# Softmax sums of a causal cross-attention block taken from ScalarE's accumulator output

## The chip, the cores and the metric

The kernel runs on one core of a Trainium2 chip. The core has a matrix engine (TensorE, PE in the profile), VectorE (DVE), ScalarE (ACT), GpSimd (POOL) and SyncE (SP, which here only issues DMAs). Each engine works through its own instructions in order, and the engines wait for each other through semaphores. The metric is the device time of one execution in microseconds (us); lower is better.

## The reference

One post-norm transformer block with cross-attention: 128 batches of 128 tokens, model width 256, 16 heads of 16, hidden width 1024, all in float32. The mask lets a token see only earlier ones (`j < i`), and the first token's attention is set to zero.

```python
q = (query @ Wq + bq).reshape(b, s, N_HEADS, D_K).transpose(0, 2, 1, 3)
k, v = ...   # the same of the context, with Wk, bk and Wv, bv
scores = jnp.einsum('bhqd,bhkd->bhqk', q, k) / jnp.sqrt(jnp.float32(D_K))
scores = jnp.where(j < i + mask, scores, NEG_INF)       # mask = 0
attn = jax.nn.softmax(scores, axis=-1)
attn = attn.at[:, :, 0, :].set(0.0)
ctx = jnp.einsum('bhqk,bhkd->bhqd', attn, v)
x = layer_norm(query + ctx @ Wo + bo, ln1_g, ln1_b)
ffn = jax.nn.relu(x @ W1 + b1) @ W2 + b2
out = layer_norm(x + ffn, ln2_g, ln2_b)
```

## The kernel before

The batches are taken two at a time: 64 pairs, `NP = 64`, one step for each. The order of the instructions on every engine is written out by hand (a manual schedule), and the kernel is a software pipeline: `step(p)` computes the scores and the softmax of pair p, the projections of pair p + 1, weighs the values of pair p - 2, and runs the feed-forward layers of pairs p - 3 and p - 4. Pairs 0 to 6 have steps of their own (`third` to `sixth` among them); `step` runs for p = 7 to 63, 57 times. After it `behind` and the last lines drain the pipeline.

The scores of a pair are held with the tokens that ask on the 128 partitions, 64 of each of the two batches. There are two tiles, both in the SBUF tile `sm`: the high one (`hi = 1`, the later 64 tokens of each batch) has 16 heads of 128 columns, the low one (`hi = 0`, the earlier 64 tokens) 16 heads of 64 columns, since an early token sees no late one. The high scores lie in PSUM banks 0 to 3, four heads in each, the low ones in banks 6, 7, 4 and 5.

In `step`, the softmax of a pair goes like this:

- VectorE adds the mask (L390 for the low tile, L743 for the high one) and takes the row maximum of each head, negated: L747, four heads at a time from each bank of the high tile, and L754 for the whole low tile.
- ScalarE makes the exponentials head by head in `exponential_by_head` (L762), 16 for the high tile out of PSUM and 16 for the low tile in place, with the negated maximum as the bias.
- `sums` on VectorE (L421, L422) reduces the exponentials to a sum for each head and row and takes the reciprocals, in three calls: heads 0 to 7 and 8 to 15 of the high tile, and all 16 heads of the low tile. GpSimd multiplies the exponentials by the reciprocals (L423).
- VectorE transposes the weights in blocks (L436, three calls of `turn`), and SyncE's DMAs (`bring`, L451) carry the blocks to their places in `pT`, which `weigh` reads two steps later.

In VectorE's own order the step is: masks and maxima, the residual sum L538 with its statistics (L525, L526), the three calls of `sums`, the transpose of the normalised tokens `x` of pair p - 2 (`turn_x1`, L663), the transposes of the next tokens (L247, twice), the first `turn`, the five additions of the second feed-forward layer (`sum_of_seven`, L823 and L831), two more calls of `turn`, and the statistics of the second norm (L525, L526). Then the masks of the next step follow.

In ScalarE's order it is: `cxT` (L505), the 32 exponentials, the query projection (L272), the first norm's `x` (L554), the keys (L291), the values (L311, L316), the second norm (L591), and the hidden layer's eight ReLUs in pairs (L707).

TensorE's order is: the scores (L376), the projections of queries (L261), attention output (L512), keys (L261) and values (L301), the second feed-forward layer as seven products (L794), the first one (L699), and the weighing of the values (L483, L493).

Of the kernel before, what the change touches and what calls it, by code (L numbers as in the profile page):

```python
# [8 lines left out]
F32 = mybir.dt.float32  # L9
AF = mybir.ActivationFunctionType  # L10
ALU = mybir.AluOpType
AX = mybir.AxisListType

P = 128
# [5 lines left out]
def tile_cross_attention_block(  # L20
# [22 lines left out]
    nc = tc.nc  # L43
# [3 lines left out]
    H = 16  # L47
# [20 lines left out]
    small = ctx.enter_context(tc.tile_pool(name="small", bufs=2))  # L68
# [182 lines left out]
    def add_bo(p):  # L251
        st = states[p]
        st["xb"] = proj.tile([P, 2, D], F32, tag="xb", name=f"xb_{p}")
        nc.gpsimd.tensor_tensor(
            st["xb"], tokens_of[p // 2][:, p % 2 * 2 : p % 2 * 2 + 2], bov_r[:, None, :].to_broadcast([P, 2, D]), ALU.add
        )
# [102 lines left out]
    def scores_both(p):  # L359

        st = states[p]
        for hi in range(2):
            st["sps", hi] = [
                at_bank(r if hi else (6, 7, 4, 5)[r], f"pss{hi}_{p}_{r}") for r in range(NS)
            ]
            room(p, hi)
        one, two = (0, 1), (2, 3)
        for strips, hi, m in (
            (two, 0, 0), (one, 1, 0), (two, 0, 1), (one, 1, 1),
            (two, 1, 0), (two, 1, 1), (one, 0, 0), (one, 0, 1),  # L370
        ):
            n = P if hi else HP
            for s in range(2):
                for r in strips:
                    strip, first = slice(32 * r, 32 * r + 32), s * P
                    nc.tensor.matmul(  # L376
                        st["sps", hi][r][
                            s * HP : (s + 1) * HP, m * 2 * n : (m + 1) * 2 * n
                        ].rearrange("p (e j) -> p e j", e=2),
                        st["qT"][strip, m, first + hi * HP : first + hi * HP + HP],  # L380
                        st["kT"][strip, m, :, first : first + n],
                        start=True, stop=True,
                    )
# [29 lines left out]
    def sums(p, hi, part):  # L413

        st = states[p]
        sm = st["sm", hi]
        n = sm.shape[2]
        su = small.tile([P, H], F32, tag=f"su{hi}", name=f"su{hi}_{p}_{part.start}")
        rs = small.tile([P, H], F32, tag=f"rs{hi}", name=f"rs{hi}_{p}_{part.start}")
        su, rs = su[:, part], rs[:, part]  # L420
        nc.vector.tensor_reduce(su, sm[:, part, :], AX.X, ALU.add)  # L421
        nc.vector.reciprocal(rs, su)  # L422
        nc.gpsimd.tensor_tensor(  # L423
            sm[:, part, :], sm[:, part, :],
            rs[:, :, None].to_broadcast([P, part.stop - part.start, n]), ALU.mult,
        )
# [46 lines left out]
    def weigh(p):  # L473

        st = states[p]
        pT = st.pop("pT")
        pc = at_bank(7, f"pc_{p}") if p > 1 else bank(f"pc_{p}")

        for m in range(KC):
            for s in range(2):  # L480
                at = (m * 2 + s) * P
                for j in range(NS):
                    nc.tensor.matmul(  # L483
                        pc[32 * j : 32 * j + 32, at : at + HP],
                        st["vd"][:, s, 4 * m + j].rearrange("p e d -> p (e d)"),
                        pT[:, 2 * s : 2 * s + 2, H + 2 * j + m, :],
                        start=True, stop=True,
                    )
            for s in range(2):
                at = (m * 2 + s) * P  # L490
                for e in range(2):
                    for j in range(NS):
                        nc.tensor.matmul(  # L493
                            pc[32 * j : 32 * j + 32, at + HP : at + P],
                            st["vz"][:, s, 4 * m + j, 2 * e : 2 * e + 2, :].rearrange(
                                "p e d -> p (e d)"
                            ),
                            pT[:, 2 * s : 2 * s + 2, 4 * j + 2 * m + e, :],
                            start=(e == 0), stop=(e == 1),
                        )  # L500
        st["pc"] = pc

    def context(p):
        pc = states[p].pop("pc").rearrange("p (u i) -> p u i", i=P)
        nc.scalar.copy(cxT.rearrange("p m s i -> p (m s) i")[:, :, 1:], pc[:, :, 1:])  # L505
# [81 lines left out]
    def norm2(p):  # L587
        st = states[p]
        t2, sd, nb = st["t2"], st["sd", 2], st["nb", 2]
        for s in range(2):  # L590
            nc.scalar.activation(  # L591
                t2[:, s], t2[:, s], AF.Identity, bias=nb[:, s], scale=sd[:, s]
            )

    def finish(p):
        t2 = states[p]["t2"]
        nc.gpsimd.tensor_tensor(t2, t2, g2_r[:, None, :].to_broadcast([P, 2, D]), ALU.mult)
        nc.gpsimd.tensor_tensor(t2, t2, be2_r[:, None, :].to_broadcast([P, 2, D]), ALU.add)
# [6 lines left out]
    def store(p):  # L605
        nc.sync.dma_start(
            out[2 * p : 2 * p + 2].rearrange("b p d -> p b d"), states.pop(p)["t2"]
        )
# [144 lines left out]
        st = states[p]  # L753
        nc.vector.tensor_reduce(st["nmx", 0], st["sm", 0], AX.X, ALU.max, negate=True)  # L754

    def exponential_by_head(p, hi, heads):

        st = states[p]
        sm, nmx = st["sm", hi], st["nmx", hi]
        for h in heads:  # L760
            src = st["sps", 1][h // 4][:, h % 4 * P : h % 4 * P + P] if hi else sm[:, h, :]
            nc.scalar.activation(sm[:, h, :], src, AF.Exp, bias=nmx[:, h : h + 1], scale=1.0)  # L762

    wt = const.tile([P, 4, FC // 2, P], F32, tag="wt", name="wt")

# [8 lines left out]
    def combine_hidden(p, engines):  # L774

        st = states[p]
        h = st["hT"].rearrange("p (k e) (s t) -> p e s k t", e=2, s=2)
        hs = st["hS"] = ffn.tile([P, 4, FC // 2, P], F32, tag="hS", name=f"hS_{p}", bufs=1)
        one, two = engines
        one.tensor_tensor(hs[:, 0], h[:, 0, 1], h[:, 1, 1], ALU.add)  # L780
        two.tensor_tensor(hs[:, 2], h[:, 0, 0], h[:, 0, 1], ALU.subtract)
        one.tensor_tensor(hs[:, 1], hs[:, 0], h[:, 0, 0], ALU.subtract)
        two.tensor_tensor(hs[:, 3], h[:, 1, 0], hs[:, 1], ALU.subtract)
# [68 lines left out]
    for which, first in (("c", c_first[:, 0:2]), ("x", tokens_of[0][:, 0:2])):  # L852
        st = states[0]
# [17 lines left out]
    for m in range(KC):  # L871
# [6 lines left out]
        for e in range(2):  # L878
            if m == 0:
                nc.scalar.activation(  # L880
                    st["kT"][:, m, e, :], pk[:, :TP], AF.Identity,
                    bias=bkh[:, m, e : e + 1], scale=half[:, e : e + 1],
# [9 lines left out]
    for m in range(KC):  # L892
# [6 lines left out]
        if m == 0:  # L899
            nc.scalar.activation(  # L900
                st["qT"][:, m, :], pq[:, :TP], AF.Identity,
                bias=bqs_c[:, m : m + 1], scale=QSCALE,
# [11 lines left out]
    for which, first in (("x", tokens_of[0][:, 2:4]), ("c", c_first[:, 2:4])):  # L914
        st = states[1]
# [59 lines left out]
    def load_ahead(p):  # L975
        if p % 2 == 0 and p + 4 < NP:
            load([p + 4, p + 5], "x")
        if p % 2 == 1:
            if p + 3 < NP:
                load([p + 3, p + 4], "c")  # L980
            if 3 < p < NP - 1:
                load_tokens((p + 1) // 2)
# [137 lines left out]
    ONES, TWOS = range(HH), range(HH, H)  # L1120
# [91 lines left out]
    def step(p):  # L1212
        last = p == NP - 1
        weigh(p - 2)
        context(p - 2)
        scores_both(p)
        if p == 7:
            norm2(p - 6)
        combine_hidden(p - 4, POOL_ALONE)
        if p == 7:  # L1220
            finish(p - 6)
            store(p - 6)
        add_bo(p - 1)
        load_ahead(p)
        mask(p, 0, B)
        if last:
            mask(p, 0, A)
        mask_high(p, A)
        exponential_by_head(p, 1, ONES)
        mask_high(p, B)  # L1230
        exponential_by_head(p, 1, TWOS)
        if not last:
            mask(p, 0, A)
        low_maximum(p)
        exponential_by_head(p, 0, range(H))
        if not last:
            queries(p + 1)
        attention_out(p - 2)
        attention_sum(p - 2)
        attention_stats(p - 2)  # L1240
        shift(p - 2, 1)
        norm1(p - 2)
        if not last:
            keys(p + 1)
        values(p)
        values_out(p)
        norm2(p - 5)
        sums(p, 1, ONE)
        sums(p, 1, TWO)
        sums(p, 0, ALL)  # L1250
        turn_x1(p - 2)
        residual1(p - 3)
        second_by_seven(p - 4)
        hidden(p - 3, range(FC))
        if p + 2 < NP:
            tokens(p + 2, "x")
            tokens(p + 2, "c")
        turn(p, 1, 0)
        sum_of_seven(p - 4)
        turn(p, 1, 1)  # L1260
        turn(p, 0, 0)
        bring(p, nc.sync, LATE_FIRST[: len(EVERY) // (1 + last)])
        finish(p - 5)
        store(p - 5)
        stats(p - 4, states[p - 4]["t2"], 2)
        scale_and_shift(p - 4)
# [6 lines left out]
    for p in range(7, NP):  # L1273
        step(p)
# [25 lines left out]
    p = NP - 1  # L1300
# [16 lines left out]
    st = states[NP - 1]  # L1317
# [53 lines left out]
```

## Time and profile before

| | |
|---|---|
| time, two runs | 1526.21 and 1532.23 us, median 1529.22 |
| the profiled execution | 1528.67 us, its span 1527.0 us |
| TensorE matmul busy | 1514.3 us |
| VectorE busy | 1332.4 us |
| GpSimd busy | 1255.9 us |
| ScalarE busy | 1118.3 us |
| exponentials by head, L762 | 944 of 128 columns and 944 of 64 columns |
| sums, L421 | 192, of which 171 (3 in each of 57 steps) are in `step` |

The profile is of one execution. A busy time is the time in which an engine had an instruction in work; an engine that is in work for all of the span sets its length, while idle time of another engine costs nothing. In a list of groups, each row gives line, engine and operation, written and read tiles, shapes and count, and then busy time, mean duration of one in ns, and the idle time of the engine just before them with what ended it. In a timeline, a row gives start, duration, engine, line, operation and count of merged instructions, with idle time before it in brackets. Instructions of ScalarE overlap: the next one starts before the one in front has ended, so the distance from start to start is shorter than a duration.

### The profile page before, as it was taken

How to read it: one execution, taken by the hardware profiler on the slowest of the kernel's cores; microseconds unless marked ns; L12 is line 12 of the kernel's file. 1: busy time of each engine (PE TensorE's matmuls, PEld its weight loads, DVE VectorE, ACT ScalarE, POOL GpSimd, SP SyncE). 2: the span in 40 equal slices, each digit the busy share in tenths (PEclk: the TensorE clock that was granted, in tenths of full speed). 3: DMA queues.
4: the chain of work that ended last, by engine and by line, in shares of the span. 5: the costliest groups of instructions: out<-in, count | busy, mean ns of one | idle time of the engine just before them, and what ended most of it. 6: DMA issues, size and time to landing. Idle time of an engine off the chain costs nothing.

```text
span 1527.0 us, 47892 instructions
## 1 busy us (share of the span) xinstructions
PE 1514.3 (99%) x17926; PEld 1360.6 (89%) x17926; DVE 1332.4 (87%) x2498; ACT 1118.3 (73%) x3391; POOL 1255.9 (82%) x1282
## 2 busy tenths in 40 slices
PE   8999999999999999999999999999999999999998
PEld 7788998998989989989989899899899898998997
DVE  7989988988988988889889889889898898898885
ACT  5668777877877877778778778777777787787752
POOL 6876988888888888888888888888888888888883
PEclk9999999999999999999999999999999999999999
DMA  9356665555656656655556666566566566564441
GB/s 192 87 120 141 154 156 132 135 136 132 143 139 138 143 120 141 148 132 135 137 134 142 145 134 136 132 136 148 134 136 138 128 141 147 133 144 109 115 112 49
DMA packets 415285, 204.24 MB, mean 134 GB/s; under 512 B 282448, under 2 KB 383056, under 8 KB 415056
## 3 DMA queue, kind: packets, MB, share of 16 engines
q1 hardware_dynamic: 412768, 199.34, 56.7%
q8 instruction: 144, 2.36, 0.7%
q10 hardware_dynamic: 2288, 1.85, 0.5%
q14 instruction: 85, 0.70, 0.2%
HBM read 70.26 MB, written 33.29 MB: 68 GB/s over the span
## 4 chain that ended last, share of the span: by engine, by line
PE 94%; DVE 3%; POOL 1%; DMA 1%; issue 1%; ACT 0%; SPq 0%; POOLq 0%; DVEq 0%
PE ph L699 28%; PE py L794 14%; PE pz L794 10%; PE pq L261 7%; PE po L512 7%; PE pv L301 7%; PE pk L261 7%; PE pss L376 6%; PE pc L493 4%; PE pc L483 2%; DVE tb L436 1%; PE py L719 0%; DMA x1t<-tbx 0%; DVE sm L390 0%; DVE su L421 0%
## 5 line engine op out<-in xcount | busy, mean ns | idle before, releaser
L699 PE MATMUL ph<-x1T,w 128*128 128x256 f32 x2048 | 453.6, 380 | 0.7 <-DMA x1T<-x1t 0.7
L699 PEld LDWEIGHTS ph<-x1T,w 128*128 128x128 f32 x2048 | 385.0, 190 | 50.9 <-issue 1.2
L423 POOL TENSOR_TENSOR sm<-sm,rs 128x1024 f32<-128x1024 f32 x192 | 359.3, 1898 | 3.9 <-DVE rs L422 3.3
L762 ACT ACTIVATE sm<-pss,nmx 128x128 f32<-128x128 f32 x944 | 249.9, 414 | 127.3 <-DMA pT<-tb 81.0
L707 ACT ACTIVATE hT<-ph,b1e_c 128x256 f32<-128x256 f32 x504 | 209.1, 467 | 171.3 <-PE ph L699 161.3
L762 ACT ACTIVATE sm<-sm,nmx 128x64 f32<-128x64 f32 x944 | 232.2, 337 | 5.1 <-DVE nmx L754 0.3
L421 DVE TENSOR_REDUCE su<-sm 128x8 f32<-128x1024 f32 (+1 forms) x192 | 225.8, 1176 | 4.0 <-ACT sm L409 3.8
L436 DVE STREAM_TRANSPOSE tb<-sm 128x1024 f32<-128x1024 f32 x186 | 221.0, 1214 | 0.0
L390 DVE TENSOR_TENSOR sm<-pss,neg 128x256 f32<-128x256 f32 (+1 forms) x276 | 108.2, 435 | 121.2 <-PE pss L376 115.4
L532 POOL TENSOR_SCALAR ve<-mv 128x2 f32<-128x2 f32 x127 | 28.7, 226 | 191.7 <-DVE mv L526 190.9
L794 PE MATMUL py<-wt,hS 128*128 128x128 f32 x1440 | 170.6, 275 | 0.0
L794 PEld LDWEIGHTS py<-wt,hS 128*128 128x128 f32 x1440 | 165.7, 192 | 0.0
L747 DVE TENSOR_REDUCE nmx<-pss 128x4 f32<-128x512 f32 x236 | 150.8, 680 | 0.0
L261 PE MATMUL pq<-xT,wq 128*128 128x256 f32 x504 | 125.5, 392 | 0.5 <-DVE sm L390 0.5
L291 ACT ACTIVATE kT<-pk,bkh,half 128x256 f32<-128x256 f32 x252 | 120.3, 558 | 4.0 <-PE pk L261 4.0
L512 PE MATMUL po<-wo,cxT 128*128 128x256 f32 x512 | 121.3, 380 | 0.7 <-ACT cxT L505 0.7
L301 PE MATMUL pv<-wv,cT 128*128 128x256 f32 x512 | 121.0, 380 | 0.0
L261 PE MATMUL pk<-cT,wk 128*128 128x256 f32 x504 | 119.2, 380 | 0.0
L512 PEld LDWEIGHTS po<-wo,cxT 128*128 128x128 f32 x512 | 97.1, 190 | 14.3 <-ACT cxT L505 1.2
L261 PEld LDWEIGHTS pq<-xT,wq 128*128 128x128 f32 x504 | 90.9, 190 | 20.8 <-issue 9.6
L301 PEld LDWEIGHTS pv<-wv,cT 128*128 128x128 f32 x512 | 97.4, 190 | 13.0
L261 PEld LDWEIGHTS pk<-cT,wk 128*128 128x128 f32 x504 | 95.9, 190 | 13.0 <-issue 0.2
(135 smaller groups left out, 2966.6 us busy)
## 6 DMA issues: line engine op xcount, KB each, us to landing
pT<-tb SPq DMA_DIRECT2D x976, 96.0 KB
x1t<-tbx SPq DMA_DIRECT2D x252, 64.0 KB
x1T<-x1t SPq DMA_DIRECT2D x63, 256.0 KB
out_dram<-t SPq DMA_DIRECT2D x63, 256.0 KB
xb<-in_x_dram SPq DMA_DIRECT2D x124, 128.0 KB
cb<-in_ctx_dram SPq DMA_DIRECT2D x124, 128.0 KB
x<-in_x_dram SPq DMA_DIRECT2D x31, 512.0 KB
w<-in_L_xattn_W_dram SPq DMA_DIRECT2D x2, 1024.0 KB
```

The lines of the kernel that those rows point to most:

```text
L261: nc.tensor.matmul(ps[:, m * TP : (m + 1) * TP], w[:, k, m * P : (m + 1) * P], src[:, k, :], start=(k == 0), stop=(k == KC - 1),)
L291: nc.scalar.activation(st["kT"][:, m, e, :], pk[:, m * TP : (m + 1) * TP], AF.Identity, bias=bkh[:, m, e : e + 1], scale=half[:, e : e + 1],)
L301: nc.tensor.matmul(pv[:, s * D : (s + 1) * D], st["cT"][:, k, s * P : (s + 1) * P], wv[:, k, :], start=(k == 0), stop=(k == KC - 1),)
L421: nc.vector.tensor_reduce(su, sm[:, part, :], AX.X, ALU.add)
L423: nc.gpsimd.tensor_tensor(sm[:, part, :], sm[:, part, :], rs[:, :, None].to_broadcast([P, part.stop - part.start, n]), ALU.mult,)
L436: nc.vector.transpose(st["tb"][:, :, at : at + 256].rearrange("p j (n a) -> p n j a", a=32), st["sm", hi].rearrange("p h j -> p (h j)")[:, ...
L512: nc.tensor.matmul(po[:, s * D : (s + 1) * D], cxT[:, k, s, :], wo[:, k, :], start=(k == 0), stop=(k == KC - 1),)
L699: nc.tensor.matmul(ph[:, i * TP : (i + 1) * TP].rearrange("p (s i a) -> p s i a", s=2, a=32), w1[:, k, (f + i) * P : (f + i + 1) * P], st[ ...
L707: nc.scalar.activation(st["hT"][:, f + i, :], ph[:, i * TP : (i + 1) * TP], AF.Relu, bias=(b1e_c if p else b1_c)[:, f + i : f + i + 1], sc ...
L747: nc.vector.tensor_reduce(st["nmx", 1][:, 4 * r : 4 * r + 4], st["sps", 1][r].rearrange("p (n j) -> p n j", j=P), AX.X, ALU.max, negate=True,)
L762: nc.scalar.activation(sm[:, h, :], src, AF.Exp, bias=nmx[:, h : h + 1], scale=1.0)
L794: nc.tensor.matmul(out, left(k), right(k), start=(k == 0), stop=(k == FC // 2 - 1))
```

## The change

In `step`, the 32 exponentials of a pair also write the sum of their output along the row: each call gets an accumulator output, one column for each head in a new small tile `sa1` (high) or `sa0` (low). `sums` finds that tile in the pair's state, leaves out VectorE's reduction and makes only the reciprocals from it. Steps 5 and 6 (`fall_in`, `sixth`) also use `exponential_by_head`, without the accumulator output, and keep VectorE's reduction, as do pairs 0 to 4. The order of all other instructions stays as it is.

```diff
@@ sums
-        su = small.tile([P, H], F32, tag=f"su{hi}", name=f"su{hi}_{p}_{part.start}")
         rs = small.tile([P, H], F32, tag=f"rs{hi}", name=f"rs{hi}_{p}_{part.start}")
-        su, rs = su[:, part], rs[:, part]
-        nc.vector.tensor_reduce(su, sm[:, part, :], AX.X, ALU.add)
+        if ("su", hi) in st:
+            su, rs = st["su", hi][:, part], rs[:, part]
+        else:
+            su = small.tile([P, H], F32, tag=f"su{hi}", name=f"su{hi}_{p}_{part.start}")
+            su, rs = su[:, part], rs[:, part]
+            nc.vector.tensor_reduce(su, sm[:, part, :], AX.X, ALU.add)
         nc.vector.reciprocal(rs, su)
@@ exponential_by_head
-    def exponential_by_head(p, hi, heads):
+    def exponential_by_head(p, hi, heads, summed=False):
         st = states[p]
+        if summed and ("su", hi) not in st:
+            st["su", hi] = small.tile([P, H], F32, tag=f"sa{hi}", name=f"sa{hi}_{p}")
         sm, nmx = st["sm", hi], st["nmx", hi]
         for h in heads:
             src = st["sps", 1][h // 4][:, h % 4 * P : h % 4 * P + P] if hi else sm[:, h, :]
-            nc.scalar.activation(sm[:, h, :], src, AF.Exp, bias=nmx[:, h : h + 1], scale=1.0)
+            nc.scalar.activation(sm[:, h, :], src, AF.Exp, bias=nmx[:, h : h + 1], scale=1.0, **(
+                {"accum_out": st["su", hi][:, h : h + 1]} if summed else {}
+            ))
@@ step
-        exponential_by_head(p, 1, ONES)
+        exponential_by_head(p, 1, ONES, True)
         mask_high(p, B)
-        exponential_by_head(p, 1, TWOS)
+        exponential_by_head(p, 1, TWOS, True)
...
-        exponential_by_head(p, 0, range(H))
+        exponential_by_head(p, 0, range(H), True)
```

## The prediction, made before the changed kernel ran

> **What bounds the kernel now.** I read the page's busy times and clock first, then one step in the windows view, then the chain's rows, the waits, and at last the timelines of ScalarE and VectorE through that step.
>
> ```profile
> PE 1514.3 (99%) x17926; PEld 1360.6 (89%) x17926; DVE 1332.4 (87%) x2498; ACT 1118.3 (73%) x3391; POOL 1255.9 (82%) x1282
> PEclk9999999999999999999999999999999999999999
> ```
>
> ```profile
> core 0: us, PE busy (x) PEld busy (x) DVE busy (x) ACT busy (x) POOL busy (x), PEclk, DMA share, GB/s
> 402.25:425.54 23.29, 23.29 (x296) 21.08 (x285) 20.66 (x40) 17.74 (x55) 19.64 (x21) 1.00 0.55 125
> sum 46.58, PE 46.58 PEld 42.17 DVE 41.34 ACT 35.28 POOL 39.23; mean PE 23.29 PEld 21.08 DVE 20.67 ACT 17.64 POOL 19.62
> ```
>
> TensorE is the bound: 99% busy in the whole, at its full granted clock, and in one step (the stretch from one mask to the next) busy in all 23.29 us. The same layer starts that much apart in the chain that ended last (416.42 - 393.13):
>
> ```profile
> 393.13 6.91 PE ph L699 x32
> 416.42 6.91 PE ph L699 x32
> ```
>
> So the shares alone say two things: taking work from VectorE wins nothing while TensorE has no gap, and ScalarE has 23.29 - 17.64 = 5.65 us of idle time in a step for work that is added. The second is too generous, since idle time counts only if it lies where the added work can use it. That is read from the order of things:
>
> ```profile
> 404.35 4.23 ACT L762 ACTIVATE sm<-pss,nmx 128x128 f32<-128x128 f32 x16 [2.13 <-DMA pT<-tb]
> 408.67 3.93 ACT L762 ACTIVATE sm<-sm,nmx 128x64 f32<-128x64 f32 x16
> 412.51 0.81 ACT L272 ACTIVATE qT<-pq,bqs_c 128x256 f32<-128x256 f32 x2
> 413.22 1.08 ACT L554 ACTIVATE x<-t,nb,sd 128x256 f32<-128x256 f32 x2
> ...
> 419.91 0.84 ACT L707 ACTIVATE hT<-ph,b1e_c 128x256 f32<-128x256 f32 x2 [0.81 <-PE ph L699]
> ```
>
> ```profile
> 402.25 0.76 DVE L390 TENSOR_TENSOR sm<-pss,neg 128x256 f32<-128x256 f32 x2 [2.12 <-PE pss L376]
> ...
> 403.58 1.28 DVE L747 TENSOR_REDUCE nmx<-pss 128x4 f32<-128x512 f32 x2
> ...
> 407.42 1.22 DVE L754 TENSOR_REDUCE nmx<-sm 128x16 f32<-128x1024 f32 x1
> ...
> 410.36 1.19 DVE L421 TENSOR_REDUCE su<-sm 128x8 f32<-128x1024 f32 x1
> 411.58 0.20 DVE L422 RECIPROCAL rs<-su 128x8 f32<-128x8 f32 x1
> ...
> 414.22 0.25 DVE L422 RECIPROCAL rs<-su 128x16 f32<-128x16 f32 x1
> 414.39 0.65 DVE L663 STREAM_TRANSPOSE tbx<-x 128x512 f32<-128x512 f32 x1
> ...
> 423.24 0.18 DVE L526 BATCH_NORM_AGGREGATE mv<-bs 128x2 f32<-128x6 f32 x1
> 425.54 0.76 DVE L390 TENSOR_TENSOR sm<-pss,neg 128x256 f32<-128x256 f32 x2 [2.12 <-PE pss L376]
> ```
>
> There is a ring through both engines, once around in each step: VectorE's masks and first maximum (402.25 to about 404.2) release ScalarE's exponentials; behind these in ScalarE's order stand the query copies and the norm `x` (L554, done at 413.22 + 1.08 = 414.30); for `x` VectorE waits with L663, which starts at 414.39; behind L663 VectorE has work without a gap up to 423.42; and then come the masks of the next step. The bracket in front of the first exponential names a DMA, but those transfers are of the pair two steps back; the maximum from L747 is what came last. The only slack in the ring is VectorE's 2.12 us in front of the masks, where it waits for the scores. It is there in nearly every step:
>
> ```profile
> DVE sm L390 <- PE pss L376: 115.4, 57, 3.2
> ```
>
> 115.4 / 57 = 2.02 us a step. A second, smaller slack lies inside the exponentials. Starting at 404.35, the last of the 16 high ones starts at 404.35 + 4.23 - 0.41 = 408.17, so the distance from start to start is 3.82 / 15 = 0.254 us and the low ones could start at 408.42. They start at 408.67, right after the low maximum (407.42 + 1.22 = 408.64): 0.25 us. Ring slack together: 2.37 us. The durations used here are these:
>
> ```profile
> L762 ACT ACTIVATE sm<-pss,nmx 128x128 f32<-128x128 f32 x944 | 249.9, 414 | 127.3 <-DMA pT<-tb 81.0 <-DVE nmx L747 42.2 <-POOL hS L781 2.2
> L762 ACT ACTIVATE sm<-sm,nmx 128x64 f32<-128x64 f32 x944 | 232.2, 337 | 5.1 <-DVE nmx L754 0.3
> L421 DVE TENSOR_REDUCE su<-sm 128x8 f32<-128x1024 f32 x128 | 150.9, 1179 | 2.6 <-ACT sm L409 2.6
> L421 DVE TENSOR_REDUCE su<-sm 128x16 f32<-128x1024 f32 x64 | 75.0, 1171 | 1.4 <-ACT sm L409 1.2
> L141 ACT ACTIVATE table<-power 128x2 f32<-128x2 f32 x1 | 0.2, 203 | 0.0
> ```
>
> **What the change removes.** In each of 57 steps three reductions: 2 x 1.179 + 1.171 = 3.53 us of VectorE, 57 x 3.53 = 201 us in all. I cost this gain at nothing. VectorE is not the bound, and the reductions lie between 410.36 and 414.2, just where the ring goes through ScalarE: with them gone VectorE reaches L663 at about 411 and waits there for `x`, which is ready at 414.30 as before. They were in the shade of the exponentials. Below nothing there is one possible gain: the query projection starts when a mask has freed its bank, and a mean of 392 ns against 380 ns for the keys' says that this costs something.
>
> ```profile
> L261 PE MATMUL pq<-xT,wq 128*128 128x256 f32 x504 | 125.5, 392 | 0.5 <-DVE sm L390 0.5
> L261 PE MATMUL pk<-cT,wk 128*128 128x256 f32 x504 | 119.2, 380 | 0.0
> ```
>
> That is 504 x 12 ns = 6 us at most, and nothing here moves the masks ahead of their scores, so I leave it out.
>
> **What it adds.** In the compiled program ScalarE's stream is longer by 1,824 entries, 57 x 32: behind each exponential stands one that reads the accumulator out. No such entry is in this trace, so its price d, from start to start, is bounded. From above by the smallest ACTIVATE there is, the 128x2 one, at its full 203 ns. From below by the same less the most that two neighbours overlap: the high exponentials take 414 ns at 254 ns apart, 160 ns, so 43 ns. The low ones, which read and write SBUF, take 337 ns at (3.93 - 0.34) / 15 = 240 ns apart and overlap by 97 ns, which gives 203 - 97 = 106 ns. I take 106 ns: a read-out writes SBUF, has no bias operand as the 128x2 ACTIVATE has none, and is short as that one is, so this row and this overlap are the nearest.
>
> Sum on ScalarE: 32 x 0.106 = 3.39 us a step, in the 8.2 us from 404.35 to 412.5 and all of it in the ring. Ring slack takes 2.37, so a step grows by 1.02 us to 24.31. 57 x 1.02 = 58 us; against the profiled execution's own 1528.67 us (span 1527.0) that gives 1587 us. The median of the runs shown, 1529.22, is half a microsecond above that execution, which is less than the runs are apart.
>
> The Trainium skill, "ScalarE: Activation LUTs", section "What ACT_TABLE_LOAD costs", gives an ACTIVATE with immediate operands 186 ns plus 0.833 ns an element, and an overlap of about 93 ns; the 203 ns of the 128x2 row and the 97 ns of the low exponentials stand close to both. By it a read-out of one element would be an estimated 94 ns, and the sum would come to 57 x (3.01 - 2.37) = 36 us, thus 1565 us.
>
> **What it moves, and the waits it adds.** The three reciprocals now wait for the read-outs of heads 7, 15 and the last low head, with all of VectorE's later work behind them. The last one ends about 0.35 us after the last exponential, and L663 behind it waits longer, for `x`; no extra price. GpSimd's multiplications (L423) wait for the reciprocals; the third one feeds the last of the three transposes, and has this cover:
>
> ```profile
> 412.11 5.61 POOL L423 TENSOR_TENSOR sm<-sm,rs 128x1024 f32<-128x1024 f32 x3
> 420.00 2.37 DVE L436 STREAM_TRANSPOSE tb<-sm 128x1024 f32<-128x1024 f32 x2
> ```
>
> It ends at 417.72 and its transpose starts near 421.2, and both move with the exponentials. On TensorE the keys and values wait until heads 0 to 3 and 4 to 7 have left banks 0 and 1; at d = 106 ns heads 4 to 7 end 8 x 0.106 = 0.85 us later, about 407.4, before the values start:
>
> ```profile
> 408.28 1.89 PE L301 MATMUL pv<-wv,cT 128*128 128x256 f32 x8
> ```
>
> The ReLUs of the hidden layer, now 0.8 us apart for TensorE's sake, can run without those gaps and catch up. SyncE's DMAs are issued later with the transposes; what they bring is read one or two steps on.
>
> **Rivals.** First, on the other side: the read-out is hidden. It decides at d = 2.37 / 32 = 74 ns. Below it TensorE keeps its 23.29 us and the time stays at 1529 us, or 1523 with the gain of the query projection. For it speaks the 43 ns bound, and that a read-out has no input to fetch; against it that the whole slack must suffice for 32 of them.
>
> Second, the read-out serialises: it starts when the exponential has ended wholly, and the next exponential when the read-out has. Each then costs 203 ns and the lost overlap, 363 ns (high) and 300 ns (low): 16 x 0.363 + 16 x 0.300 = 10.6 us, and 57 x (10.6 - 2.37) = 469 us, thus 1998 us. For it speaks that a sum is complete only when its last element is through; against it that neighbours overlap in all rows shown.
>
> Third, the change is less than it says, and the sums stay on VectorE: the built program has 171 VectorE instructions fewer, 3 x 57, so I give it nothing.
>
> **How the numbers follow.** My forecast, d between 74 and 203 ns with 106 the likeliest, gets 0.68; at the upper bound it is 57 x (6.50 - 2.37) = 235 us, 1764 us. Hidden gets 0.21, serialised 0.10, and a gain that I don't see 0.01. By 2%, about what a measurement of this kernel can tell from no change, is 31 us, 0.54 us a step, d = 91 ns; I put 0.06 of the forecast's chance between 74 and 91. Slower is thus 0.62 + 0.10 = 0.72, within 2% 0.06 + 0.21 = 0.27, faster 0.01. The range goes from the hidden case at the edge of the runs, 1525, to the upper bound, 1764; serialised and faster are left out, 0.11. The forecast alone has 1529 to 1764.
>
> **What would show it.** Right: between exponentials a new row on ScalarE, 1,824 of it; VectorE's busy time down by some 200 us; no more wait of VectorE for scores in front of L390, but one of about 3 us and more in front of L663 or the last reciprocal for ScalarE; TensorE with gaps of about 1 us a step in front of the query projection or the scores, released by VectorE. Wrong: a step of still 23.29 us with the 2.12 shrunk (hidden), the exponentials' distance above 540 ns (serialised), or gaps of TensorE that ScalarE releases itself, at the keys, values or hidden layer (then the ring is not what binds).

## The result and the profile after

The changed kernel takes 1574.47 us (median of two runs, 1574.42 to 1574.51) against 1529.22 us: a ratio of 1.0299, with an interval from 1.0263 to 1.0335 (the quotient of the two medians is 1.0296). It is slower. The profiled execution of it has a span of 1572.5 us, 45.5 us more than the one before. The page's busy times and its shares of the chain that ended last, with the shares of the kernel before as a third line:

```profile
PE 1526.7 (97%) x17926; PEld 1360.6 (87%) x17926; DVE 1138.8 (72%) x2327; ACT 1260.1 (80%) x5215; POOL 1258.4 (80%) x1282
PE 75%; ACT 10%; DVE 9%; issue 2%; DMA 2%; SPq 1%; POOL 0%; DVEq 0%; POOLq 0%; ACTq 0%
PE 94%; DVE 3%; POOL 1%; DMA 1%; issue 1%; ACT 0%; SPq 0%; POOLq 0%; DVEq 0%
```

VectorE lost 193.6 us of work (1332.4 - 1138.8), and yet the kernel is longer: TensorE has gaps now, and ScalarE and VectorE have come into the chain that ended last, with 10% and 9% where they had 0% and 3%. ScalarE has 1,824 instructions more. The list of groups names them, one behind each exponential of the 57 steps:

```profile
L767 ACT ACTIVATION_READ_ACCUMULATOR sm<-pss,nmx 128x1 f32 x912 | 222.0, 243 | 0.0
L767 ACT ACTIVATION_READ_ACCUMULATOR sm<-sm,nmx 128x1 f32 x912 | 234.0, 257 | 0.0
```

Their mean durations, 243 and 257 ns, are not their price, since ScalarE's instructions overlap. The price shows in the timeline, as what a read-out adds to the distance from one exponential to the next. This is the start of the 32, the passage from the high to the low ones, and what follows:

```profile
701.15 0.37 ACT L767 ACTIVATE sm<-pss,nmx 128x128 f32<-128x128 f32 x1 [3.15 <-DMA pT<-tb]
701.42 0.19 ACT L767 ACTIVATION_READ_ACCUMULATOR sm<-pss,nmx 128x1 f32 x1
701.51 0.36 ACT L767 ACTIVATE sm<-pss,nmx 128x128 f32<-128x128 f32 x1
...
706.64 0.43 ACT L767 ACTIVATE sm<-sm,nmx 128x64 f32<-128x64 f32 x1
706.88 0.29 ACT L767 ACTIVATION_READ_ACCUMULATOR sm<-sm,nmx 128x1 f32 x1
706.98 0.43 ACT L767 ACTIVATE sm<-sm,nmx 128x64 f32<-128x64 f32 x1
...
711.94 0.86 ACT L272 ACTIVATE qT<-pq,bqs_c 128x256 f32<-128x256 f32 x2
712.66 1.14 ACT L557 ACTIVATE x<-t,nb,sd 128x256 f32<-128x256 f32 x2
```

The next exponential starts 0.09 us after its neighbour's read-out (701.42 to 701.51), though that read-out is on record for 0.19. Over the steps between 200 and 1400 us the median distance from exponential to exponential went from 0.249 to 0.342 us (high) and from 0.239 to 0.331 us (low): a read-out costs 92 to 93 ns. VectorE in the same step:

```profile
699.05 0.76 DVE L390 TENSOR_TENSOR sm<-pss,neg 128x256 f32<-128x256 f32 x2 [0.19 <-issue]
...
704.22 1.22 DVE L757 TENSOR_REDUCE nmx<-sm 128x16 f32<-128x1024 f32 x1
...
707.17 0.24 DVE L425 RECIPROCAL rs<-sa 128x8 f32<-128x8 f32 x2
712.12 0.25 DVE L425 RECIPROCAL rs<-sa 128x16 f32<-128x16 f32 x1 [4.72 <-ACT sm L767]
713.83 0.71 DVE L666 STREAM_TRANSPOSE tbx<-x 128x512 f32<-128x512 f32 x1 [1.45 <-ACT x L557]
...
722.73 0.18 DVE L529 BATCH_NORM_AGGREGATE mv<-bs 128x2 f32<-128x6 f32 x1
723.11 0.76 DVE L390 TENSOR_TENSOR sm<-pss,neg 128x256 f32<-128x256 f32 x2 [0.19 <-PE pss L376]
...
747.15 0.76 DVE L390 TENSOR_TENSOR sm<-pss,neg 128x256 f32<-128x256 f32 x2 [0.19 <-PE pss L376]
```

Where VectorE had its reductions it now stands idle, 4.72 us for the last sum and 1.45 us for `x`, and its wait in front of the masks has shrunk from 2.12 to 0.19 us. TensorE in turn waits for VectorE's masks to free a bank, as in this row of its timeline:

```profile
747.63 1.56 PE L261 MATMUL pq<-xT,wq 128*128 128x256 f32 x6 [0.68 <-DVE sm L390]
```

From mask to mask a step takes 24.05 us in the median (here 723.11 - 699.05 = 24.06 and 747.15 - 723.11 = 24.04), 0.76 more than before. Each part of the ring gives its share of that, in medians over the steps: from the masks to the first low exponential 1.17 us more, the low exponentials 1.43 more, from the end of the last one to L666 0.03 more, the VectorE work behind it 0.05 more, and the wait for the scores 1.92 less.

### The profile page after: what moved, and what is told of

Read it like the earlier page. It is cut to its first block, busy times and chain, and to the rows that moved or that the text cites. A ratio compares the mean times of both kernels' runs of the same rounds, so it can differ in the third digit from the quotient of the medians.

```text
span 1572.5 us, 49429 instructions
## 1 busy us (share of the span) xinstructions
PE 1526.7 (97%) x17926; PEld 1360.6 (87%) x17926; DVE 1138.8 (72%) x2327; ACT 1260.1 (80%) x5215; POOL 1258.4 (80%) x1282
## 4 chain that ended last, share of the span: by engine, by line
PE 75%; ACT 10%; DVE 9%; issue 2%; DMA 2%; SPq 1%; POOL 0%; DVEq 0%; POOLq 0%; ACTq 0%
PE ph L702 22%; PE py L801 11%; PE pz L801 8%; ACT sm L767 8%; PE pq L261 6%; PE po L515 5%; PE pv L301 5%; PE pk L261 5%; PE pss L376 5%; PE pc L496 3%; DVE tb L439 3%; PE pc L486 2%; DVE sm L390 2%; DVE t L830 1%; SPq L454 1%
## 5 line engine op out<-in xcount | busy, mean ns | idle before, releaser
L767 ACT ACTIVATE sm<-pss,nmx 128x128 f32<-128x128 f32 x944 | 327.8, 403 | 176.9 <-DMA pT<-tb 126.7
L767 ACT ACTIVATE sm<-sm,nmx 128x64 f32<-128x64 f32 x944 | 313.5, 403 | 0.3 <-DVE nmx L757 0.3
L767 ACT ACTIVATION_READ_ACCUMULATOR sm<-sm,nmx 128x1 f32 x912 | 234.0, 257 | 0.0
L425 DVE RECIPROCAL rs<-sa 128x8 f32<-128x8 f32 x171 | 28.1, 192 | 270.2 <-ACT sm L767 270.2
L767 ACT ACTIVATION_READ_ACCUMULATOR sm<-pss,nmx 128x1 f32 x912 | 222.0, 243 | 0.0
L710 ACT ACTIVATE hT<-ph,b1e_c 128x256 f32<-128x256 f32 x504 | 192.3, 475 | 32.5 <-PE ph L702 22.6
L600 POOL TENSOR_TENSOR t<-t,g_r 128x512 f32<-128x512 f32 x62 | 78.9, 1273 | 60.0 <-ACT t L594 60.0
```

The lines of the kernel that those rows point to most:

```text
L710: nc.scalar.activation(st["hT"][:, f + i, :], ph[:, i * TP : (i + 1) * TP], AF.Relu, bias=(b1e_c if p else b1_c)[:, f + i : f + i + 1], sc ...
```

## The experiments

The theory: 32 read-outs of 92 ns lie in a ring through ScalarE and VectorE, which had 2.18 us of slack a step (2.12 - 0.19 = 1.93 in front of the masks, about 0.25 in front of the low exponentials); only what goes beyond the slack costs time, and VectorE's relief is worth nothing. The rivals: ScalarE's added time counts wherever it lies, in proportion; or the loss is VectorE's wait for ScalarE's last sum; or VectorE's relief did pay, and covered a larger loss. Each edit is shown against the changed kernel. Ratios are to the kernel before, run on the same chip in each set.

**Half of the read-outs.** On the high tile alone, and on the low tile alone (the edit of the first; the second takes `True` from the two high calls):

```diff
-        exponential_by_head(p, 0, range(H), True)
+        exponential_by_head(p, 0, range(H))
```

> Accumulator output on the 16 high exponentials alone, 16 read-outs a step; the low tile's sum stays on VectorE. Ring theory: 16 x 0.092 = 1.47 us, of which 0.25 goes into the wait for the low maximum and 1.22 into VectorE's 1.93 us of slack: hidden, 1529 us, a ratio of 1.00 to the kernel before. Rival, ScalarE's added time counts wherever it lies: half of the change's loss of 45 us, about 1552. Rival, the loss is the wait of the last reciprocal for ScalarE: that wait is gone here, 1529 as well.

> Accumulator output on the 16 low exponentials alone; the high tile's two sums stay on VectorE. Ring theory: 16 x 0.092 = 1.47 us against 1.93 us of slack: hidden, 1529 us. Rival, added time counts wherever it lies: about 1552. Rival, the wait of the last reciprocal for ScalarE is the loss: it is still there, so 1574.

Measured: 1529.21 us for the high tile, 1.0011 (1.0002 to 1.0021), and 1529.55 us for the low tile, 1.0015 (1.0005 to 1.0024). The steps are 23.29 us apart in both, and the slack in front of the masks has shrunk just as the sum says, to 2.12 - 1.22 = 0.90 and 2.12 - 1.47 = 0.65. Of the two rows for each kernel the bracket is to be read, and the distance of the two starts. With the high tile alone:

```profile
634.00 0.76 DVE L390 TENSOR_TENSOR sm<-pss,neg 128x256 f32<-128x256 f32 x2 [0.89 <-PE pss L376]
...
657.29 0.76 DVE L390 TENSOR_TENSOR sm<-pss,neg 128x256 f32<-128x256 f32 x2 [0.89 <-PE pss L376]
```

With the low tile alone:

```profile
635.86 0.76 DVE L390 TENSOR_TENSOR sm<-pss,neg 128x256 f32<-128x256 f32 x2 [0.62 <-PE pss L376]
...
647.73 0.25 DVE L425 RECIPROCAL rs<-sa 128x16 f32<-128x16 f32 x1 [1.02 <-ACT sm L767]
...
659.15 0.76 DVE L390 TENSOR_TENSOR sm<-pss,neg 128x256 f32<-128x256 f32 x2 [0.64 <-PE pss L376]
```

So time does not grow in proportion, and a last reciprocal that waits for ScalarE, here 1.02 us, is not by itself a loss.

**Three quarters of them.**

```diff
-        exponential_by_head(p, 0, range(H), True)
+        exponential_by_head(p, 0, ONES, True)
+        exponential_by_head(p, 0, TWOS)
...
             su, rs = st["su", hi][:, part], rs[:, part]
+            if not hi:
+                nc.vector.tensor_reduce(su[:, HH:], sm[:, HH:, :], AX.X, ALU.add)
```

> 24 read-outs a step: the 16 high heads and low heads 0 to 7; VectorE sums low heads 8 to 15. Ring theory: 24 x 0.092 = 2.21 us against 2.18 us of slack, so a step grows by 0.03 us and the time is 1531 us; the loss of the change lies in its last eight read-outs. Rival, added time counts wherever it lies: three quarters of the 45 us, about 1563.

Measured: 1535.01 us, 1.0045 (1.0028 to 1.0062). Here the slack is just used up, and a step takes 660.57 - 637.24 = 23.33 us:

```profile
637.24 0.76 DVE L390 TENSOR_TENSOR sm<-pss,neg 128x256 f32<-128x256 f32 x2 [0.19 <-PE pss L376]
...
649.59 0.69 DVE L422 TENSOR_REDUCE sa<-sm 128x8 f32<-128x512 f32 x1 [4.00 <-ACT sm L769]
...
660.57 0.76 DVE L390 TENSOR_TENSOR sm<-pss,neg 128x256 f32<-128x256 f32 x2 [0.19 <-PE pss L376]
```

Nearly all of the change's loss sits in its last eight read-outs. The time is 4 us above the expectation of 1531; about 1.5 of these lie behind the last step's masks. The rest is eleven steps of 23.5 to 23.8 us, in which VectorE waits 0.35 to 0.66 us for the scores; why they come late there stays open.

**The place of a read-out.** Four more accumulator outputs a step that nobody uses, once on the query copies and the norm `x`, once on the key copies, which stand in ScalarE's order right behind them:

```diff
-                bias=bqs_c[:, m : m + 1], scale=QSCALE,
+                bias=bqs_c[:, m : m + 1], scale=QSCALE, **extra(p > 7, m)
...
-                    bias=bkh[:, m, e : e + 1], scale=half[:, e : e + 1],
+                    bias=bkh[:, m, e : e + 1], scale=half[:, e : e + 1], **extra(p > 7, 2 * m + e)
```

The first pair of lines is the one kernel (with the same on `x`), the second the other; `extra` gives an accumulator output into a spare column.

> The change, with four more accumulator outputs a step that nobody uses, on ScalarE instructions inside the ring: the two query copies and the two norms x. Ring theory: 4 x 0.092 = 0.37 us a step, 57 x 0.37 = 21 us on top of the change: 1595 us. Rival, ScalarE has room left since it is busy 20 of 24 us: 1574.

> The change, with the same four additional accumulator outputs a step on instructions that stand behind the ring's exit to VectorE: the four key copies. Ring theory: ScalarE's gaps before the next exponentials take them, 1574 us as the change. Rival, added time of ScalarE counts wherever it lies: 1595, as with the four inside the ring.

Measured: 1593.29 us inside the ring, 1.0432 (1.0417 to 1.0448), and 1573.78 us behind its exit, 1.0302 (1.0285 to 1.0319). The same four read-outs cost 19 us in one place and nothing in the other, while ScalarE's busy time is 1279.5 us in both. In the first a step takes 659.46 - 635.04 = 24.42 us, which is 24.05 + 4 x 0.092:

```profile
635.04 0.75 DVE L395 TENSOR_TENSOR sm<-pss,neg 128x256 f32<-128x256 f32 x2 [0.19 <-PE pss L381]
...
659.46 0.75 DVE L395 TENSOR_TENSOR sm<-pss,neg 128x256 f32<-128x256 f32 x2 [0.19 <-PE pss L381]
```

In the second, 650.69 - 626.65 = 24.04 us:

```profile
626.65 0.75 DVE L395 TENSOR_TENSOR sm<-pss,neg 128x256 f32<-128x256 f32 x2 [0.19 <-PE pss L381]
...
650.69 0.42 DVE L395 TENSOR_TENSOR sm<-pss,neg 128x256 f32<-128x256 f32 x1 [0.19 <-PE pss L381]
```

**What VectorE's relief is worth.** Once VectorE makes its sums again beside the accumulator outputs, and once there are neither, so that the reciprocals are taken of the negated maxima and this kernel leaves the softmax sums out:

```diff
-        if ("su", hi) in st:
-            su, rs = st["su", hi][:, part], rs[:, part]
-        else:
-            su = small.tile([P, H], F32, tag=f"su{hi}", name=f"su{hi}_{p}_{part.start}")
-            su, rs = su[:, part], rs[:, part]
-            nc.vector.tensor_reduce(su, sm[:, part, :], AX.X, ALU.add)
+        su = small.tile([P, H], F32, tag=f"su{hi}", name=f"su{hi}_{p}_{part.start}")
+        su, rs = su[:, part], rs[:, part]
+        nc.vector.tensor_reduce(su, sm[:, part, :], AX.X, ALU.add)
```

> Accumulator outputs as in the change, but VectorE also makes all its sums again and uses those; the accumulated sums are not used. Ring theory: VectorE's first two reductions and most of the third lie in the shade of the exponentials (the third ends with its reciprocal about 1.4 us after the last exponential, and x is ready 1.8 us after it), so the time is that of the change, 1574 us: what the change took off VectorE was worth nothing. Rival, VectorE's relief did pay and covered a larger loss: clearly above 1574, by up to 3.5 us a step, 1775.

```diff
-            st["su", hi] = small.tile([P, H], F32, tag=f"sa{hi}", name=f"sa{hi}_{p}")
+            st["su", hi] = st["nmx", hi]
...
-            nc.scalar.activation(sm[:, h, :], src, AF.Exp, bias=nmx[:, h : h + 1], scale=1.0, **(
-                {"accum_out": st["su", hi][:, h : h + 1]} if summed else {}
-            ))
+            nc.scalar.activation(sm[:, h, :], src, AF.Exp, bias=nmx[:, h : h + 1], scale=1.0, )
```

> No accumulator output and no reduction: the reciprocals are taken of another tile of that shape (the negated maxima), so the softmax sums are left out of the computation. Ring theory: 1529 us, at the least 1523 if the query projection's wait goes; TensorE has no gap that VectorE's 201 us could close. Rival, VectorE's relief is worth something by itself: below 1515.

Measured: 1572.18 us with both, 1.0293 (1.0278 to 1.0308), and 1527.89 us with neither, 1.0000 (0.9990 to 1.0009). With both, the last reduction still ends before `x` is ready, so that L663 waits 0.19 us:

```profile
640.12 1.22 DVE L421 TENSOR_REDUCE su<-sm 128x16 f32<-128x1024 f32 x1 [2.23 <-ACT sm L764]
641.38 0.25 DVE L422 RECIPROCAL rs<-su 128x16 f32<-128x16 f32 x1
641.82 0.71 DVE L663 STREAM_TRANSPOSE tbx<-x 128x512 f32<-128x512 f32 x1 [0.19 <-ACT x L554]
```

With neither, the wait in front of the masks is 2.12 us as in the kernel before, and what VectorE saved stands as idle time in front of the transpose of `x`:

```profile
644.58 0.71 DVE L666 STREAM_TRANSPOSE tbx<-x 128x512 f32<-128x512 f32 x1 [3.62 <-ACT x L557]
...
655.78 0.75 DVE L390 TENSOR_TENSOR sm<-pss,neg 128x256 f32<-128x256 f32 x2 [2.12 <-PE pss L376]
```

**The ring cut, with all 32 read-outs.**

```diff
-        exponential_by_head(p, 0, range(H), True)
+        exponential_by_head(p, 0, range(HH), True)
...
         norm1(p - 2)
+        exponential_by_head(p, 0, range(HH, H), True)
...
         sums(p, 1, TWO)
-        sums(p, 0, ALL)
         turn_x1(p - 2)
+        if p + 2 < NP:
+            tokens(p + 2, "x")
+            tokens(p + 2, "c")
+        sums(p, 0, ALL)
...
         hidden(p - 3, range(FC))
-        if p + 2 < NP:
-            tokens(p + 2, "x")
-            tokens(p + 2, "c")
```

> All 32 read-outs stay, but the ring is cut: on ScalarE the query copies and the norm x stand between the eighth and the ninth low exponential, and on VectorE the transposes of x and of the next tokens stand ahead of the low tile's reciprocal. Ring theory: VectorE's work behind the last exponential shrinks by the three transposes (1.9 us) and the 1.8 us of query copies and norm no longer follow it but come before it; the ring falls below TensorE's 23.29 us and the time returns to 1529 us, no further, since TensorE has no gap to win. Rival, ScalarE's added time as such is the loss: 1574, since ScalarE does the same work.

Measured: 1532.51 us, 1.0029 (1.0019 to 1.0040). ScalarE does all its added work (1266.1 us busy), and the steps are back at 656.75 - 633.46 = 23.29 us:

```profile
633.46 0.76 DVE L390 TENSOR_TENSOR sm<-pss,neg 128x256 f32<-128x256 f32 x2 [1.08 <-PE pss L376]
...
645.61 0.71 DVE L666 STREAM_TRANSPOSE tbx<-x 128x512 f32<-128x512 f32 x1 [3.81 <-ACT x L557]
648.25 0.25 DVE L425 RECIPROCAL rs<-sa 128x16 f32<-128x16 f32 x1 [0.73 <-ACT sm L767]
...
656.75 0.75 DVE L390 TENSOR_TENSOR sm<-pss,neg 128x256 f32<-128x256 f32 x2 [1.08 <-PE pss L376]
```

Left over are 4.7 us. To place them, the last step alone was put back into the order of the kernel before, with VectorE's sums:

```diff
-        exponential_by_head(p, 1, ONES, True)
+        exponential_by_head(p, 1, ONES, not last)
...
-        exponential_by_head(p, 0, range(H), True)
+        exponential_by_head(p, 0, range(H if last else HH), not last)
...
         norm1(p - 2)
         if not last:
+            exponential_by_head(p, 0, range(HH, H), True)
...
-        sums(p, 0, ALL)
+        if last:
+            sums(p, 0, ALL)
         turn_x1(p - 2)
...
+        if not last:
+            sums(p, 0, ALL)
```

> The reordered kernel with all read-outs, but the last of the 57 steps (pair 63) in the order of the kernel before and with VectorE's sums. The reordered kernel took 1532.5 us against 1527.8 us beside it although its steps were 23.29 us apart, as before; from its last step's masks to its end there were 79.5 us against 75.6 us in the kernel before. Theory: those 4 us are the last pair's own softmax, whose exponentials nothing hides when the pipeline drains; then 1528 to 1529 us here, a ratio of 1.00. Rival: they come from somewhere in the steps; then 1532 still.

Measured: 1528.90 us, 1.0009 (1.0000 to 1.0018). The place was right, the mechanism was another. In the last step the values lie in bank 4, the bank of the hidden layer's third product as well, so TensorE waits for ScalarE's copies of the values (L316). This is its timeline in the reordered kernel:

```profile
1459.23 3.62 PE L702 MATMUL ph<-x1T,w 128*128 128x256 f32 x16
1464.86 5.41 PE L702 MATMUL ph<-x1T,w 128*128 128x256 f32 x16 [2.01 <-ACT vd L316]
```

The first 16 matmuls take 3.62 us and the second 16, behind the wait, 5.41. 2.01 us of waiting and 1.79 us of slower matmuls are most of the 4 us by which this kernel is longer behind the last masks.

No version here beats the kernel before. What the runs show is why none does: with the ring out of the way TensorE is back at 23.29 us a step without a gap (busy in all of the 69.58 us from 1380.00 to 1449.58), and nothing in this change takes work from TensorE.

## Why the prediction was right

- **The bound.** TensorE's gapless step was the limit before, and VectorE's relief, costed at nothing, was worth nothing: 1527.89 against 1527.99 us with the sums left out, and a ratio of 1.0293 against the change's 1.0299 with the sums made twice. The possible 6 us of the query projection did not come either.
- **The ring and its exit.** The step read it as masks, exponentials, `x`, L663, VectorE's remaining work, masks. Four read-outs ahead of the exit cost 19 us, four behind it none, and the reordering of the exit gave the steps back their 23.29 us. TensorE's gaps are of the kind that was named, in front of the query projection and released by VectorE, 0.68 us in the row above where about 1 us was forecast.
- **The slack.** 2.37 us were forecast; 32 x 0.092 = 2.94 us of read-outs lengthened the step by 0.76, so 2.18 were there. The missing 0.19 us is the wait in front of the masks that never goes. In the changed kernel it is 0.19 us in 54 of the 58 steps that begin with this mask, also where the profile names nothing that was waited for (`issue`, as at 699.05). Before the mask VectorE's queue works through four entries that wait for earlier transfers, one after the other. Ahead of the mask at 723.11 these transfers had all landed by 720.81, and still each entry takes 21 to 50 ns, some 0.1 us from start to start. The row of that line names them, with the shortest, median and longest duration in ns and the first and last start:

```profile
L390 DVEq EVENT_SEMAPHORE  x4: 21/50/50, 722.7 to 723.0; - x4
```

- **The price of a read-out.** 106 ns were taken, from bounds of 43 and 203; it is 92 to 93 ns. This is the term that was mis-sized: it makes the sum 57 x (3.39 - 2.94) = 26 us too high. The slack, taken 0.19 us too large, makes it 57 x 0.19 = 11 us too low, and the last step, 4 us, is missing. That the forecast lies only 12.5 us too high is in part luck, since these errors pull against each other: with the measured price and the forecast slack the sum would have been 57 x (2.94 - 2.37) = 32 us, hardly more than the 31 us at which the prediction begins to call it slower, and with the measured slack 57 x 0.76 = 43 us, 1572 us. The estimate from the Trainium skill, "ScalarE: Activation LUTs", section "What ACT_TABLE_LOAD costs", 94 ns, was the better one, and the trace agrees with it as a distance from start to start. It does not agree with its parts: the read-outs are 243 and 257 ns long on record, where the figures of the Trainium skill give an estimated 187. The sum by that estimate came out 9 us low, for the slack and the last step.
- **The last step** was not foreseen. Of the 45.5 us some 42 lie between the first and the last step's masks (1493.06 - 145.53 against 1451.43 - 146.02), and 3.9 behind these, 79.44 against 75.57 us, by the bank that `values` shares with the hidden layer there: as in the reordered kernel, TensorE waits 2.00 us for L316, and the matmuls behind the wait take 1.79 us longer. These are the rows of the windows view from the last masks on, in the changed kernel and then in the one before. Behind the length stand the busy times of PE, PEld, DVE, ACT and POOL, each with its count, and then the granted clock, the DMA share and GB/s:

```profile
1493.06:1572.50 79.44, 72.03 (x608) 65.00 (x608) 46.32 (x101) 33.41 (x116) 43.76 (x51) 0.96 0.28 80
```

```profile
1451.43:1527.00 75.57, 70.07 (x608) 64.00 (x608) 50.18 (x104) 30.46 (x84) 42.30 (x50) 0.99 0.30 80
```

- **The rivals.** Hidden decides at 2.18 / 32 = 68 ns, and the price was above it; 24 read-outs, 2.21 us, sit on the edge as the sum says. Serialised is out: neighbours stay 0.34 us apart. The sums did leave VectorE: it has 2,327 instructions where it had 2,498, 171 fewer.

## What to carry to other kernels

An engine's idle share doesn't say what it can take on: ScalarE had 5.65 us idle in a step and was given 2.94, and still the kernel lost 45 us, since the work went into a ring with 2.18 us of slack. Follow the ring around once, find the one place where it waits, and subtract what is added from that. Work taken off an engine that waits elsewhere in the same ring brings nothing, and where added work must stay, moving the ring's exit ahead of it can make it free.

## What the runs showed of the hardware

An accumulator output is a second instruction on ScalarE, on record for 243 to 257 ns and costing 92 to 93 ns from start to start, for 64 and for 128 columns alike.

TensorE's granted clock fell after a wait of 2.0 us in some kernels, and not in others. In the reordered kernel's last step, the windows view with the granted clock in the third column from the end gives 0.63 for 4.5 us that begin within that wait (1462.85 to 1464.86), and 16 matmuls took 5.41 us instead of 3.62:

```profile
1464.00:1468.50 4.50, 3.64 (x9) 2.94 (x10) 4.25 (x7) 3.45 (x10) 4.41 (x4) 0.63 0.25 73
```

The changed kernel and the one with read-outs on the key copies did the same after 2.00 us (0.61 over 4.4 us in both). But with the sums made twice, and with the four read-outs inside the ring, the same matmuls came behind a wait as long or longer and took 3.72 us, at a granted clock of 1.00:

```profile
1508.60 3.72 PE L699 MATMUL ph<-x1T,w 128*128 128x256 f32 x16 [2.00 <-ACT vd L316]
1529.26 3.72 PE L708 MATMUL ph<-x1T,w 128*128 128x256 f32 x16 [2.18 <-ACT vd L321]
```

So the length of the wait alone does not decide it, and what does stays open. The Trainium skill, "TensorE: Matmul & The Clock Gate", section "Why this matters for your kernels", asks for no idle gaps over about 3 us between bursts of matmuls. Here gaps of 2.0 us were enough in three kernels. The 0.7 us gaps in the changed kernel's steps left the clock at 1.00.
